# Strassen's seven products in the gated section of a decoder block with two attentions, with the last batch transposed on TensorE

## The chip, the core and the metric

The kernel runs on one core of a Trainium2 chip, in float32, as one launch. The metric is the device time of an execution in microseconds; the time of a kernel is the median of its runs. Five engines run their own queues of instructions: TensorE (PE, matrix products), VectorE (DVE), ScalarE (ACT), GpSimd (POOL) and SyncE (SP), which here issues all transfers.

## The reference, cut to what matters

There are 16 batches of 128 tokens with 512 features, and as many context tokens. A decoder block comes first: self-attention with 16 heads of 32, cross-attention on the context, and an MLP of 512 to 2048 to 512. A gated cross-attention follows, which is where the change lies. Its inputs are the block's result x and the context, normalised with a gain and an offset:

```python
Q, K, V = x @ Wq.T, a @ Wk.T, a @ Wv.T          # a = layer_norm(ctx); 16 heads of 32
scores = einsum(Q, K) * scale                   # scale = 1 / sqrt(32)
scores = where(mask, scores, -inf)              # mask: batch x key
out = softmax(scores) @ V
return x + tanh(gate) * (out @ Wo.T)
```

For a batch without a single valid key the softmax is undefined, and the result of the reference is not a number there. The inputs of the runs have all keys valid.

## The kernel before, in words

**Groups and sections.** The 16 batches form four groups of four (512 tokens). Each attention is done a group at a time, in sections: A0 to A3 (self), B0 to B3 (cross), then the MLP in 16 steps (4 groups by 4 quarters of the hidden width), then D0 to D3 (gated). x stays in SBUF, one tile for each group (`x[g]`).

**Steps.** `attend` runs a section in 16 steps, four for each batch; later stages of a batch lie some steps behind. A unit is one of the four parts of a batch's heads, 128x512 numbers. At the first step of a batch `scores` makes all four units on TensorE, into four PSUM banks called sc. Then, unit by unit, DVE adds the mask and moves the scores to SBUF (`scale_unit`) and takes a minimum (`least_unit`), ACT makes four exponentials with sums (`exp_unit`), DVE inverts the sums and POOL multiplies (`norm_unit`), DVE transposes in squares of 32 and SP stores the unit in device memory (`turn_unit`, the tile `away`), and SP loads pairs of units back in the order that the mixing wants (`receive_pair`, the tile `pT`). Eight to eleven steps after its scores, `mix` multiplies a batch's probabilities with the values (the bank `av`, copied by ACT into `mT`) and `out_project` makes the output chunk (`mo`), added into x by `finish`, which also stores the result.

**Beside the attention.** While section i attends, TensorE makes q, k and v of section i+1 (`jobs`, at the steps in PRODUCTS, three of four) and the inputs of section i+2 are made ready (`prepare`: hidden states and normalised context, transposed through device memory). A chunk is four matmuls of 128x512 into one bank, of which two (`pt`) and two single ones (`mm0`, `mm1`) are used in turn. In the self-attention, for three groups, the same projections are made by `block_product`: Strassen's method with seven products on a 2x2 split of both factors, each of four matmuls of 128x256, from sums of weight blocks and of token blocks made before (`left_blocks`, `right_blocks`), with copies and adds that build the four quarters of the result. The MLP works in that way, too (`H_ORDER` and `O_ORDER` give the order of the seven products). The q, k and v of D0 are chunks made before the gated sections begin.

**The gated sections.** D1 to D3 get q, k and v by plain chunks. The scale goes into q as ACT moves it out of its bank, and a column `mcol` of ones (not a number, where a batch has no valid key) into v. The mixed values of D0 to D2 are kept in SBUF, and their twelve output chunks are made beside the last section and shortly after its last scores, from the list `deferred`, since the last section has no section behind it whose projections could fill TensorE:

```python
return plan((deferred, [1, 3, 5, 7, 9, 11, 16, 17, 19]))
```

**Order.** Every engine's instructions stay in the order in which the program issues them (`InOrder`). Within a step that is: loads of probabilities, scores, what the step before left for later (`due`: evictions put off with `afterwards`), jobs, output chunk, mixing, preparations, transpose, normalisation, minimum and exponentials, masks of scores. All instructions are recorded in one helper, so every row of the trace is at line L49, and rows are told apart by the names of their tiles: `sc`, `av`, `mo`, `mm_q`, `mm_k`, `mm_v`, with the letter of the section (`_D`).

Of the kernel before, what the change touches and what calls it, by code (L numbers as in the profile page):

```python
# [16 lines left out]
P = 128  # L17
# [35 lines left out]
def decoder_then_gated_cross_attention(ctx: ExitStack, tc: tile.TileContext, a: dict, out: bass.AP):  # L53
# [120 lines left out]


    mrow8 = cpool.tile([NB, S], U8, tag="mrow8", name="mrow8")
    mrow = cpool.tile([NB, S], F32, tag="mrow", name="mrow")
    some = cpool.tile([NB, 1], F32, tag="some", name="some")
    mcol = cpool.tile([P, NB], F32, tag="mcol", name="mcol")
    gate = cpool.tile([P, 1], F32, tag="gate", name="gate")  # L180

    def load_small():
        nc.sync.dma_start(out=ms1, in_=a["mask_1x1xSxS2_fc1"][0, 0])
        nc.sync.dma_start(out=mrow8, in_=a["mask_BxS2_bf1"])
        nc.sync.dma_start(out=gate, in_=a["L1_xattn_gate"].partition_broadcast(P))

    def key_masks():
        nc.vector.tensor_copy(mrow, mrow8)
        nc.vector.tensor_reduce(some, mrow, AX.X, ALU.max)
        nc.vector.reciprocal(some, some)  # L190
        nc.vector.tensor_scalar(mrow, mrow, some, None, ALU.mult)
        tm = ps("mm", "tm")
        nc.tensor.transpose(tm[:, 0:NB], mrow, ident[0:NB, 0:NB])
        nc.vector.tensor_copy(mcol, tm[:, 0:NB])
# [4 lines left out]
    def small_jobs():  # L199
# [4 lines left out]
             lambda: turn_vectors(1), key_masks],  # L204
            [1, 2, 3, 8, 9, 13],
# [79 lines left out]
    def chunk_back(dst, back, k, scale=None, bias=None):  # L285

        dst, src = dst.rearrange("p (b n t) -> p b n t", b=GB, n=NQ), back[:, :, :, k].rearrange("p n b t -> p b n t")
        if scale is None:
            nc.scalar.copy(dst, src)
# [32 lines left out]
    def project_chunk(t, wt, actT, c, name, bias=None, bias0=0, bank="mm", scale=None):  # L322
# [4 lines left out]
        if bias is None:  # L327
            afterwards(
                "act", lambda: nc.scalar.copy(t[:, c], mm) if scale is None else nc.scalar.mul(t[:, c], mm, scale)
            )  # L330
# [3 lines left out]
    def values_chunk(v, wt, actT, b, name, bias_row=None, keep=None):  # L334
# [4 lines left out]
        if keep is None:  # L339
            afterwards("dve", lambda: nc.vector.tensor_tensor(v[:, b, :], mm, bias_row, ALU.add))  # L340
        else:
            afterwards("act", lambda: nc.scalar.mul(v[:, b, :], mm, keep[:, b : b + 1]))
# [17 lines left out]
    def left_blocks(wt, t):  # L360
# [3 lines left out]
        s3, s2, s4 = t  # L364
        return [a11, a12, s4, a22, a21, s2, s3], [
            (s3, a11, a21, ALU.subtract), (a21, a21, a22, ALU.add), (s2, a21, a11, ALU.subtract),
# [12 lines left out]
    def block_product(out, left, right, turned, name, bias=None):  # L379

        bank = {}
        (c11, c12), (c21, c22) = out

        def product(n, tag, first):
# [10 lines left out]
            return mm.rearrange("p (o t) -> p o t", t=HF)  # L397

# [35 lines left out]

    BLOCKS = (
# [12 lines left out]
        {12: (1,), 13: (6, 2), 14: (7, 5), 15: (4, 3)},  # L448
    )
# [11 lines left out]
    class Section:  # L461
# [4 lines left out]
        deferred = v_bias = None  # L466
# [4 lines left out]
    class Batch:  # L471
        def __init__(self, sec, b):
            self.sec, self.b, self.name = sec, b, f"{sec.name}_{b}"
            self.sc, self.s, self.mn, self.sum, self.away, self.pT = {}, {}, {}, {}, {}, {}
# [18 lines left out]
    def scale_unit(bt, j):  # L493
        s = work.tile([P, NQ, KC, Q], F32, tag="s", name=f"s_{bt.name}_{j}", bufs=8)
        bt.s[j] = s
# [30 lines left out]

    def receive_pair(bt, j):
# [10 lines left out]
    def mix(bt):  # L538
# [11 lines left out]
        def mixed_out():  # L550
            if sec.v_bias is None:
                nc.scalar.copy(mT.rearrange("p c q -> p (c q)"), av)
# [27 lines left out]
    def attend(sections, ready, others, after=None):  # L580
# [11 lines left out]
        def step(k, bt=None, jobs=(), ahead=None, last=True):  # L592
# [3 lines left out]
            if pair % 2 and 0 <= pair < len(units):  # L596
# [6 lines left out]
            if m == 0 and projected:  # L603
                before = projected.popleft()
                if before.sec.deferred is None or last:
                    out_project(before)
                else:
                    before.sec.deferred.append(lambda: out_project(before))
            done = k // GB - 2
            if m == 2 and 0 <= done < len(batches):  # L610
# [4 lines left out]
            if 0 <= k - 3 < len(units):  # L615
                turn_unit(*units[k - 3])
            if 0 <= k - 2 < len(units):
# [769 lines left out]
```

## Time and profile before

| | |
|---|---|
| time, median of three runs (1202.28, 1202.28, 1206.63) | 1202.28 us |
| the profiled execution's own time | 1202.3 us |
| its span | 1200.0 us |
| TensorE: matmuls busy, weight loads busy | 1165.7 us, 772.2 us |
| DVE, ACT, POOL busy | 745.7, 581.6, 603.8 us |
| first scores of D0, first of D1, of D2, of D3 | 970.26, 1020.98, 1073.02, 1125.06 us |
| last scores | 1163.49 us |
| moved by transfers | 249.18 MB |

Times within the profile are in microseconds from the start of the span. A busy time is the sum of the durations of an engine's instructions; TensorE's overlap a little, and the ends of its matmuls are modelled, so the distances from start to start say more than durations. In a timeline row, x8 are eight records: one float32 matmul leaves two, so a chunk has eight, and so has a product of four 256-wide matmuls. A number in brackets at the end of a row is the time that the engine idled before it, with the name of what it waited for.

### The profile page before, as it was taken

To read this page: it belongs to the slowest core of one execution; us is meant where nothing else is said; L and a number is where in the kernel's file an instruction comes from. 1 tells how busy PE (TensorE), PEld (TensorE's weight loads), DVE (VectorE), ACT (ScalarE), POOL (GpSimd) and SP (SyncE) were. 2 spreads that over 40 slices of the span, in tenths; PEclk is the share of its full clock that TensorE was granted. 3 is DMA by queue.
4 is the path that set the end of the run, shared out by engine and by line. 5 is a ranking of instruction groups with operands and counts; after the bars stand their busy time and mean duration, and the time that the engine had idled before them with its cause. 6 is when DMAs were issued, how large, how long until landed. Compare 5 with 4: busy or idle time off the path is not lost. (4 is left out here: it accounts for less than half of the span.)

```text
span 1200.0 us, 20209 instructions
## 1 busy us (share of the span) xinstructions
PE 1165.7 (97%) x6707; PEld 772.2 (64%) x6707; DVE 745.7 (62%) x1444; ACT 581.6 (48%) x2038; POOL 603.8 (50%) x555
## 2 busy tenths in 40 slices
PE   7989999999999999998999999999999999999997
PEld 5867677644444444444788888888888754444443
DVE  8678979776867767865754634542532255648674
ACT  2556667666655556664231222222222256868552
POOL 6777878675757556675233524433441232324231
PEclk9999999999999999999999999999999999999999
DMA  6578778898978869697696474585457538676576
GB/s 213 159 199 218 201 207 221 222 263 211 211 212 207 233 195 245 180 270 226 217 320 203 158 268 158 184 285 190 150 206 248 171 107 225 166 203 188 160 227 183
DMA packets 317983, 249.18 MB, mean 208 GB/s; under 512 B 82932, under 2 KB 278200, under 8 KB 313016
## 3 DMA queue, kind: packets, MB, share of 16 engines
q1 hardware_dynamic: 317840, 247.89, 70.9%
q8 instruction: 53, 0.87, 0.3%
q14 instruction: 50, 0.41, 0.1%
q10 hardware_dynamic: 40, 0.01, 0.0%
HBM read 158.70 MB, written 89.13 MB: 207 GB/s over the span
## 5 line engine op out<-in xcount | busy, mean ns | idle before, releaser
L49 ACT ACTIVATE s_B<-s_B,mn_B 128x128 f32<-128x128 f32 x256 | 99.5, 391 | 82.0 <-issue 60.6
L49 POOL TENSOR_TENSOR s_D<-s_D,sum_D 128x512 f32<-128x512 f32 x64 | 66.6, 1041 | 142.1 <-DVE sum_D L49 133.8
L49 DVE TENSOR_TENSOR h<-h,h 128x512 f32<-128x512 f32 x80 | 54.9, 687 | 119.0 <-PE h L49 118.4
L49 ACT ACTIVATE s_A<-s_A,mn_A 128x128 f32<-128x128 f32 x256 | 99.5, 393 | 55.7 <-issue 37.8
L49 ACT ACTIVATE s_D<-s_D,mn_D 128x128 f32<-128x128 f32 x256 | 99.4, 390 | 42.2 <-issue 34.6
L49 ACT ACTIVATE h<-h 128x512 f32<-128x512 f32 x64 | 40.3, 630 | 158.1 <-DVE h L49 153.8
L49 POOL TENSOR_TENSOR s_B<-s_B,sum_B 128x512 f32<-128x512 f32 x64 | 67.0, 1047 | 62.7 <-DVE sum_B L49 54.8
L49 POOL TENSOR_TENSOR s_A<-s_A,sum_A 128x512 f32<-128x512 f32 x64 | 66.7, 1043 | 53.9 <-DVE sum_A L49 49.6
L49 POOL TENSOR_TENSOR s_B<-s_B,mask 128x512 f32<-128x512 f32 x64 | 81.8, 1279 | 6.2 <-DVE s_B L49 4.6
L49 POOL TENSOR_TENSOR s_A<-s_A,ma 128x512 f32<-128x512 f32 x64 | 81.8, 1278 | 5.8 <-DVE s_A L49 4.3
L49 POOL TENSOR_TENSOR sh<-h 128x512 f32<-128x512 f32 x32 | 41.5, 1298 | 53.1 <-ACT h L49 43.3
L49 POOL TENSOR_TENSOR rstd_aD<-rstd_aD,mhalf 128x1 f32<-128x1 f32 x12 | 6.6, 550 | 115.1 <-DVE rstd_aD L49 101.8
L49 PE MATMUL mo_B<-w_co,mT_B 128*128 128x512 f32 x128 | 60.7, 618 | 1.8 <-ACT mT_B L49 1.8
L49 PE MATMUL h<-T_C,w 128*128 128x256 f32 x256 | 61.1, 381 | 1.2 <-DVE h L49 1.2
L49 PE MATMUL h<-T_C,t 128*128 128x256 f32 x256 | 60.7, 380 | 1.2 <-DVE h L49 1.1
L49 PE MATMUL mo_A<-w_ao,mT_A 128*128 128x512 f32 x128 | 59.1, 604 | 1.8 <-ACT mT_A L49 1.8
L49 PE MATMUL mo_D<-w_go,mT_D 128*128 128x512 f32 x128 | 57.9, 601 | 2.9 <-ACT mT_D L49 2.9
L49 PE MATMUL h<-sx,t 128*128 128x256 f32 x256 | 60.6, 379 | 0.0
L49 PE MATMUL o<-t,h 128*128 128x256 f32 x256 | 60.5, 379 | 0.0
L49 PE MATMUL o<-w,h 128*128 128x256 f32 x256 | 60.5, 379 | 0.0
L49 PE MATMUL o<-t,sh 128*128 128x256 f32 x256 | 60.5, 379 | 0.0
L49 PE MATMUL mm_v_D<-w_gv,T_a 128*128 128x512 f32 x128 | 59.9, 616 | 0.0
(220 smaller groups left out, 2753.1 us busy)
## 6 DMA issues: line engine op xcount, KB each, us to landing
t<-kept SPq DMA_DIRECT2D x24, 1024.0 KB, 10.2
away_A<-s_A SPq DMA_DIRECT2D x64, 256.0 KB, 2.7
pT_A<-away_A SPq DMA_DIRECT2D x128, 128.0 KB, 2.9
away_B<-s_B SPq DMA_DIRECT2D x64, 256.0 KB, 3.2
pT_B<-away_B SPq DMA_DIRECT2D x128, 128.0 KB, 3.1
away_D<-s_D SPq DMA_DIRECT2D x64, 256.0 KB, 3.0
pT_D<-away_D SPq DMA_DIRECT2D x128, 128.0 KB, 2.8
w<-in_L_xattn_w_dram SPq DMA_DIRECT2D x24, 512.0 KB, 4.3
```

The costliest lines, as they stand in the source:

```text
L49: return lambda *args, **kw: self.tc.keep_in_program_order(call(*args, **kw))
```

## The change

**Projections.** q, k and v of D1 to D3 come from `block_product`, at the steps of GATED_BLOCKS. Products 1, 6 and 7 share a bank (`mm0`) and accumulate: 6 begins when ACT has copied 1 out, and 7 when it has copied 6. The sums of the weight blocks are made once: those of Wq at the end of the MLP, of Wk on DVE and of Wv on POOL in the first steps of D0. The token sums are made on POOL for each group, four of the hidden states (in `prepare`, from step 10) and four of the context (steps 0 to 3 of the section before).

**Outputs.** The output chunks of D0, D1 and D2 become one block product for each group (`added_product`, DEFERRED_BLOCKS), added straight into x: ACT copies products 1, 6 and 7 into spare tiles and POOL adds them, DVE adds the other four from their banks. D3 keeps its four chunks. tanh(gate) is multiplied into Wo while that is prepared, and `finish` is a plain addition. Mixed values of D0 and D1 are stored in device memory (eight transfers of 256 KB) and fetched back in the steps 6 to 13 of D2's attention. x of the first group is stored in device memory during the MLP and fetched back at those steps 8 to 11; in between its tile holds block sums.

**Masks.** `mcol` and `key_masks` go. For each group `find_void` makes 0/max(mask) for each batch in an MLP step, and `add_void` adds that to x on ACT, 16 times (zero, or not a number for a batch with no valid key).

**Last batch.** The four units of the last batch of D3 are turned by TensorE, four transposes of 128x128 a unit into an sc bank, and copied out by DVE (even units) and ACT (odd ones), with no transfer; its mixing comes at step 67 in place of 70 and its output chunk in the step after. In the gated sections exponentials are issued ahead of normalisations.

**Around it.** The last two of the MLP's output products change places, and a small exponential near the MLP's end makes ACT load its table there.

```diff
@@ GatedAttention.jobs
-            keep = mcol[:, g * GB : (g + 1) * GB]
-            aT, xT = self.aT, self.xT
-            out = [lambda c=c: project_chunk(self.q, w["gq"], xT, c, f"q_{n}", scale=-SCALE) for c in range(KC)]
-            out += [lambda c=c: project_chunk(self.k, w["gk"], aT, c, f"k_{n}") for c in range(KC)]
-            out += [lambda b=b: values_chunk(self.v, w["gv"], aT, b, f"v_{n}", keep=keep) for b in range(GB)]
-            return plan((out, PRODUCTS), ([mask], [7]))
+            a_sides, a_sums = right_blocks(self.aT, self.a_at)
+            products = [
+                block_product(halves(self.q), self.sides[0], self.x_sides, False, f"q_{n}"),
+                block_product(halves(self.k), self.sides[1], a_sides, False, f"k_{n}"),
+                block_product(by_quarters(self.v), self.sides[2], a_sides, True, f"v_{n}"),
+            ]
...
+            if g == 1:
+                more = (
+                    ([by_dve(o) for o in self.sums[1]], [1, 1, 2, 2]),
+                    ([by_pool(o) for o in self.sums[2]], [4, 5, 6, 7]),
+                )
+            elif g == 3:
+                more = self.deferred_start()
+            return plan(
+                *blocks_plan(products, GATED_BLOCKS), ([by_pool(o) for o in a_sums], [0, 1, 2, 3]), ([mask], [9]), *more
+            )
@@ step: products of each projection, deferred group
+    GATED_BLOCKS = (
+        {0: (1,), 1: (6, 2), 2: (7,), 3: (5,), 4: (4,), 5: (3,)},
+        {5: (1,), 6: (6,), 7: (7, 2), 8: (5,), 9: (4,), 10: (3,)},
+        {11: (1, 2), 12: (6,), 13: (7, 5), 14: (4,), 15: (3,)},
+    )
+    DEFERRED_BLOCKS = (
+        {0: (1,), 1: (6, 2), 2: (7,), 3: (4,), 4: (5,), 5: (3,)},
+        {5: (1,), 6: (6, 2), 7: (7,), 8: (4,), 9: (5,), 10: (3,)},
+        {12: (1,), 13: (6, 2), 14: (7,), 15: (4,), 16: (5,), 17: (3,)},
+    )
@@ added_product
+            if n in (1, 6, 7):
+                t = parts[0]
+                parts.rotate(-1)
+                nc.scalar.copy(t, product(n, "mm0", n == 1))
...
+            elif n == 5:
+                add(c22, product(n, "mm1", True))
@@ deferred_start: steps of D2's attention
+                ([begin_sums], [11]),
+                ([lambda: add(self.o_sums) for _ in range(4)], [11, 12, 13, 14]),
+                ([lambda: add(self.m_sums[0]) for _ in range(4)], [12, 13, 14, 15]),
@@ last batch
+    def turn_by_array(bt, j):
+        s = by_head(bt.s.pop(j)).rearrange("p c n k -> p c (n k)")
+        tp = ps("sc", f"tp_{bt.name}_{j}")
+        for c in range(KC):
+            nc.tensor.transpose(tp[:, c * S : (c + 1) * S], s[:, c], ident)
@@ void
+        def find_void(self):
+            m8, self.void = self.load_mask(), void[:, self.g * GB : (self.g + 1) * GB]
+            def make():
+                nc.vector.tensor_reduce(self.void, m8, AX.X, ALU.max)
+                nc.vector.reciprocal(self.void, self.void)
+                nc.vector.tensor_scalar(self.void, self.void, 0.0, None, ALU.mult)
+            afterwards("dve", make)
...
+        if n % GB == 3 and r == 2:
+            gates[n // GB].find_void()
@@ mlp
-        O_ORDER = (0, 1, 3, 5, 6, 4, 2)
+        O_ORDER = (0, 1, 3, 5, 6, 2, 4)
```

## The prediction

> **What bounds the kernel now.** First the busy line of the page, then TensorE's waits from 950 us on, where the gated sections lie.
>
> ```profile
> PE 1165.7 (97%) x6707; PEld 772.2 (64%) x6707; DVE 745.7 (62%) x1444; ACT 581.6 (48%) x2038; POOL 603.8 (50%) x555
> ```
> ```profile
> engine line waited for: us in total, times, longest us
> PE mo_D L49 <- ACT mT_D L49: 2.9, 2, 2.2
> PE sc_D L49 <- DVE x L49: 1.4, 1, 1.4
> PE sc_D L49 <- DVE s_D L49: 0.7, 2, 0.3
> ```
> TensorE (PE) never rests: 5.0 us of waits in 250. The time there is the sum of its matmuls, so what counts is how many there are, how wide, and which new waits come between them. Its timeline gives one gated batch and the tail:
>
> ```profile
> 1009.27 7.13 PE L49 MATMUL mm_v_D<-w_gv,T_a 128*128 128x512 f32 x16
> 1016.34 1.08 PE L49 MATMUL av_D<-pT_D,v_D__7550 128*32 128x128 f32 x32
> 1017.35 3.70 PE L49 MATMUL mm_v_D<-w_gv,T_a 128*128 128x512 f32 x8
> 1020.98 1.17 PE L49 MATMUL sc_D<-k_D,q_D 32*128 32x128 f32 x32
> ...
> 1163.49 1.17 PE L49 MATMUL sc_D<-k_D,q_D 32*128 32x128 f32 x32
> ...
> 1175.10 7.13 PE L49 MATMUL mo_D<-w_go,mT_D 128*128 128x512 f32 x16 [2.17 <-ACT mT_D L49]
> ...
> 1192.49 3.70 PE L49 MATMUL mo_D<-w_go,mT_D 128*128 128x512 f32 x8 [0.73 <-ACT mT_D L49]
> ```
> Starts repeat every 12.81 us (1008.17, 1020.98): scores 1.11, mixing 1.02, three 512-wide chunks at 3.56. The chunks are q, k and v of the next section or, after 1125.06, deferred outputs. What takes their place exists already in the self-attention, four rows of whose timeline follow. The second fence, of the same view, has a group of transposes from the kernel's start and two places at the end of the cross-attention:
>
> ```profile
> 190.47 1.89 PE L49 MATMUL mm_q_A<-sums_A,w_sq 128*128 128x256 f32 x8
> 192.20 1.89 PE L49 MATMUL mm_q_A<-T_A,sums 128*128 128x256 f32 x8
> ...
> 221.35 1.89 PE L49 MATMUL mm_k_A<-T_A,sums 128*128 128x256 f32 x8
> 224.02 1.99 PE L49 MATMUL mm_v_A<-w_sv,sums_A 128*128 128x256 f32 x8 [0.78 <-DVE k_A L49]
> ```
> ```profile
> 6.30 1.12 PE L49 MATMUL tp_A<-ident,ln_A 128*128 128x128 f32 x4 [1.73 <-DVE ln_A L49]
> ...
> 530.97 1.07 PE L49 MATMUL av_B<-pT_B,v_B 128*32 128x128 f32 x28 [2.84 <-DMA pT_B<-away_B]
> 531.96 5.40 PE L49 MATMUL mm_v_D<-w_gv,T_a 128*128 128x512 f32 x8
> ...
> 548.99 5.40 PE L49 MATMUL mo_B<-w_co,mT_B 128*128 128x512 f32 x8 [1.80 <-ACT mT_B L49]
> ```
> A product of four 256-wide matmuls starts 1.73 us after the one before. The product at 224.02 waited for the eviction of an earlier bank: 2.67 us from start to start, a loss of 0.94. (The 5.40 rows serve a rival.)
>
> **Projections by seven products.** Twelve chunks (12×3.557 = 42.7 us) become 21 products. The self-attention's section with products, 169.48 to 230.61, takes 61.13 us; less scores and mixings (four of 1.11+1.02), outputs (four of 3.54) and 0.94 of stalls, 37.5 remain, 1.786 each. That saves 5.2 per section; the plain section after it (230.61 to 295.58, 64.97) against this one gives 4.8 without the stalls. I take 5.0, three times.
>
> The Trainium skill, "TensorE: Matmul & The Clock Gate", Back-to-back issue gap, says that weight loads and matmuls together set the spacing, with 81 ns sustained at 128 columns and 131 at 512. A line through these gives an estimate of 98 at 256, three quarters of a wide one: 21 products would then take 55 us, and every section would lose some 13. The trace disagrees, 1.73 against 3.56; the measurement decides.
>
> **New waits for a bank.** Products 1, 6 and 7 accumulate in one bank, and 6 and 7 must wait until ACT has copied it. Where PE has nothing in between, it stands still: 1→6 of q and 6→7 of v in each section, 6→7 of k in the first, 1→6 of deferred group 0; eight places. The nearest row, 224.02, lost 0.94 around a 0.69 us DVE add; a 0.57 us copy (ACT, k_D) instead gives 0.82. Bounds: 0, and 0.82+1.55 if four exponentials (0.39 each) stand ahead of the copy on ACT. I take 0.82: the copy is queued ahead of that step's exponentials. Eight cost 6.6.
>
> **Sums and adds.** Per section POOL gains eight sums (1.27 each), DVE twelve adds into q, k, v (0.69) while ACT loses three copies. In 1000–1050 DVE is busy 30.8 of 50 and POOL 15.7, so this is covered; uncovered, the DVE adds would be 8.3 us a section. The query-weight sums (one POOL, three DVE) and the gate's four multiplications go to the MLP's end, beside the last products of the MLP: nothing; were they late, the first product would stand behind 3×0.69. Four key-weight sums on DVE early in section one may take 1.75 instead of 0.69 (the MLP's t<-w beside a POOL sum took 1.75); I put 0.5 on scores there (0 to 4). In steps 11 to 15 of section three POOL has two sums and a normalisation, 1.27+1.27+1.04 = 3.6 us against about 2.9 of PE work; probabilities come up to 5×0.7 late, but are wanted three steps later: +1.0 (0 to 3.5).
>
> **Start of section one.** The last two output products of the MLP are swapped, so the bank that the first scores wait for (1.42) is emptied earlier: −1.4 (0 to −1.42).
>
> **Deferred outputs.** Of these, nine groups lie between 1125.06 and the last scores: 32.0 us become 14 products at 1.786, 25.0; plus one bank wait, 0.8, and 1.0 at a score bank in the second batch, where PE has some 7.5 us of work left against 9.3 on DVE (0 to 3): −5.2. Their mixed values, and the first group's x, now go through device memory, 256 KB each; the away_D stores of that size landed in 3.0 us, and the fetches start four or more steps ahead. SP has them among the away and pT transfers; no gated wait names a DMA, so none is charged (0 to 2, were a pT to arrive late). The x parts leave in an MLP step; SP holds weight loads there (512 KB in 4.3 us), which run about 8 us ahead, against some 3 us for one part. The copies of products go into spare tiles, from where POOL adds them into x (three copies, four POOL sums and four DVE adds a group; POOL 1.27 each, 12 in 38 us where it was busy 10.5): covered, and nothing on PE waits for the sums in x but the stores.
>
> **Tail.** After the last scores PE now does seven chunks and three mixings. It will do seven products (12.5), four chunks (14.2), three mixings (3.1), scores (1.1) and 16 transposes: from tp_A, 4×1.1 = 4.4. The 2.17 wait goes, since no transfer stands ahead of the last mixing; what is late next is the copy after it, 0.73 still. With the closing add that is 36.2 against 33.5 before (1163.49 to 1196.98): +2.7 (0 to +5).
>
> **Void keys.** 16 ACT additions (0.63) and four masks with three small DVE operations each come into the MLP, in place of scales on evictions that ACT did anyway. ACT idles 153.8 us there before h<-h, so the additions are covered; each is queued behind the TensorE group that it follows and ahead of the next T and h copies, where 0.63 is under the 2.2 us that the copies idle on average (158.1 over 64). DVE's three operations take under 0.3 us each by its 128x4 rows (a reciprocal 0.17), but they wait for a DMA, and the h additions are queued behind them: see the last rival. The small key-mask operations of the start, one transpose among them, go, at no price that the waits show.
>
> **Sum.** Section one −5.0+2.5−1.4+0.5 = −3.4; two and three −5.0+1.6 each = −6.8; POOL +1.0; deferred −5.2; tail +2.7: −11.7. The profiled run took 1202.3 us, span 1200.0 and 2.3 around it, which is the median of the runs, too. So 1190.6.
>
> **Rivals.**
> *Copies hidden.* The eight waits, the lag of POOL and of the score bank all vanish (6.6+1.0+1.0+0.5): 1181.5. Against: the order of PE's work is fixed and the pairs are adjacent.
> *Copies behind exponentials.* Each of the eight waits 1.55 longer: 12.4, 1203.0, no gain. For: ACT's exponentials of a unit are consecutive. Against: the order on ACT. It decides if a unit's minimum is early, by over half a step.
> *The clock.* After 2.84 us of idle a chunk took 5.40 instead of 3.70, after 1.80 again; after 2.17 at 1175.10 it did not, nor after 0.78 at 224.02. If each of the eight short waits costs that 1.7, 13.6 come on top: 1204.2. It decides from idles near 1.8 us. The Trainium skill, same page, section "A second HAM failure mode: psum-queue depth-cycling", says that frequent short idles between groups that cycle through PSUM banks make the clock gate oscillate. By that rule the sections would run at this rival's time; no row here shows it at 0.8 us.
> *Not faster: the masks.* In each of four MLP steps DVE waits until a mask has landed. In the trace one such wait was 9.0 us:
> ```profile
>   DMA m<-in_mask_BxS_bf_dram: 9.0, 1
> ```
> If all four stood in DVE's queue like that, beyond a slack of about 2.8 us, with h evictions behind them and PE behind those, 4×6.2 = 25: 1215, slower. It decides where the mask is issued: landing over 10 us after its issue. Against: the weight loads of those steps are issued 8 us ahead of their step.
> That the change does not do what it says: 512-wide mm_q_D rows would remain and the time stay; I give it nothing, the instructions being in the program.
>
> **How the numbers follow.** 0.5% (6.0 us) is about what a measurement of this kernel can tell from no change. Forecast, 1184 to 1196: 0.55. Copies hidden: 0.13. Behind exponentials 0.10, clock 0.08: both within 0.5% for the most part. Masks 0.08. The rest, 0.06, half slower. Faster 0.73, same 0.14, slower 0.13. From 1181 to 1205 leaves out the masks and a little on either side.
>
> **What would show it.** Right: product starts 1.73 apart; mm_q_D, mm_k_D, mm_v_D with waits of 0.6 to 0.8 on ACT, eight in all; the first scores of the sections 47 to 49 us apart; last scores near 1149. Wrong: waits over 2 us at these places (exponentials), 256-wide starts over 2 us with no wait (clock), h waiting for DVE behind m in the MLP, an av_D waiting for pT_D, or sc_D for s_D at every batch.

## The result, and the profile after

Over 22 runs of each kernel the median is 1197.35 us with the change and 1202.06 us before; the ratio is 0.9963, with a 95% interval of 0.9947 to 0.9978. So the change makes the kernel faster by 4.5 us (by the ratio; the medians lie 4.7 apart), a little over a third of the 11.7 that were forecast. The interval leaves out 1, but the gain is less than the 0.5% named as what can be told from no change. The profiled execution has a span of 1195.9 us against 1200.0: 4.1 us less, in keeping with the runs, so the two traces can be laid side by side.

The busy line of the page, then TensorE's waits from 930 us on (who waited for whom: total, times, longest). Besides the names explained above, `mm_o` are the products of the deferred outputs, `parts` the spare tiles that ACT copies them into, and `gsums` sums of weight blocks:

```profile
PE 1152.9 (96%) x7010; PEld 830.0 (69%) x7010; DVE 770.5 (64%) x1493; ACT 593.6 (50%) x2061; POOL 673.4 (56%) x612
```
```profile
PE av_D L49 <- DMA pT_D<-away_D: 2.7, 2, 2.2
PE sc_D L49 <- DVE s_D L49: 2.5, 2, 2.3
PE mm_q_D L49 <- ACT q_D L49: 2.3, 3, 0.8
PE mm_o_D L49 <- DVE x L49: 2.1, 1, 2.1
PE mm_v_D L49 <- ACT v_D L49: 2.0, 3, 0.7
PE mo_D L49 <- ACT mT_D L49: 0.9, 2, 0.8
PE mm_k_D L49 <- POOL gsums L49: 0.8, 1, 0.8
PE mm_o_D L49 <- ACT parts L49: 0.8, 1, 0.8
```
TensorE is busy for 12.8 us less, and 9.1 us more of the gated part are waits: 14.1 against 5.0. Six of them (mm_q, mm_v) and the ones of mm_k and mm_o_D for parts are the forecast waits for a bank, 0.7 to 0.8 each. (The list names POOL for mm_k; ACT's copy out of that bank ended within 0.1 us of POOL's sum.) Three others are over 2 us each: a mixing that waits for its probabilities, for which nothing was charged, and scores and a product that wait for DVE, for which 0.5 and 1.0 were. Here they are in the timeline of TensorE, with what follows the first two:

```profile
982.12 0.50 PE L49 MATMUL sc_D<-k_D__7653,q_D 32*128 32x128 f32 x6
984.95 1.12 PE L49 MATMUL sc_D<-k_D__7653,q_D 32*128 32x128 f32 x26 [2.33 <-DVE s_D L49]
986.00 1.99 PE L49 MATMUL mm_q_D<-x,w_gq 128*128 128x256 f32 x8
...
1055.27 1.71 PE L49 MATMUL av_D<-pT_D,v_D 128*32 128x128 f32 x28 [2.18 <-DMA pT_D<-away_D]
1056.91 4.71 PE L49 MATMUL mm_v_D<-w_gv,T_a 128*128 128x256 f32 x16
...
1154.77 1.99 PE L49 MATMUL mm_o_D<-gsums_o,mixed 128*128 128x256 f32 x8 [2.11 <-DVE x L49]
```
The mixing at 1055.27 took 1.71 in place of 1.07, and the two products after it 4.71 in place of 3.72 as at 1005.44; the granted clock was 0.66 from 1055 to 1060. So the wait cost 2.2, and the slow clock behind it 1.6 more. By the starts of the scores, the difference stands like this:

| part | before | after | change | forecast |
|---|---|---|---|---|
| first scores of D0 at | 970.26 | 971.16 | +0.9 | 0 |
| section one (to the first scores of D1) | 50.72 | 50.02 | −0.7 | −3.4 |
| section two | 52.04 | 52.45 | +0.4 | −3.4 |
| section three | 52.04 | 49.14 | −2.9 | −2.4 |
| deferred outputs (to the last scores) | 38.43 | 34.93 | −3.5 | −5.2 |
| last scores to the end of the span | 36.51 | 38.20 | +1.7 | +2.7 |
| sum | | | −4.1 | −11.7 |

Sections one and two are where most of the gain is missing (6.5 of 7.6 us). The first scores come between 964.9 and 971.9 in all the profiles below, though most of these kernels differ in nothing ahead of them; so +0.9 there means nothing, and profiles are compared from the first scores to the end of the span: 229.7 before, 224.7 after. A profile is one execution, and in the runs below it lies up to 3.5 us from the median of its kernel (e2 above it, e11 below); differences of that size in a profile's total say little by themselves.

### The profile page after: what moved, and what is told of

Its sections match the earlier page's. It is cut to its first block, busy times and chain, and to the rows that moved or that the text cites. A ratio compares the mean times of both kernels' runs of the same rounds, so it can differ in the third digit from the quotient of the medians.

```text
span 1195.9 us, 21040 instructions
## 1 busy us (share of the span) xinstructions
PE 1152.9 (96%) x7010; PEld 830.0 (69%) x7010; DVE 770.5 (64%) x1493; ACT 593.6 (50%) x2061; POOL 673.4 (56%) x612
## 4 chain that ended last, share of the span: by engine, by line
PE 82%; DVE 5%; DMA 4%; POOL 3%; issue 3%; SPq 2%; ACT 1%; ACTq 0%; DVEq 0%; POOLq 0%
PE o L49 15%; PE h L49 14%; PE mo_A L49 5%; PE mm_v_B L49 5%; PE mm_q_B L49 5%; PE mm_k_B L49 5%; PE mo_B L49 4%; PE mm_k_A L49 3%; PE mm_q_D L49 3%; PE mm_k_D L49 3%; PE mm_v_A L49 3%; PE mm_v_D L49 3%; PE mm_o_D L49 3%; PE mm_q_A L49 3%; SPq L49 2%
## 5 line engine op out<-in xcount | busy, mean ns | idle before, releaser
L49 ACT ACTIVATE s_D<-s_D,mn_D 128x128 f32<-128x128 f32 x256 | 99.5, 391 | 27.1 <-issue 10.6
L49 PE MATMUL mm_v_B<-w_cv,T_e 128*128 128x512 f32 x128 | 57.7, 599 | 0.0
L49 PE MATMUL mm_k_B<-T_e,w_ck 128*128 128x512 f32 x128 | 57.3, 595 | 0.0
```

The source lines that it names most:

```text
L49: return lambda *args, **kw: self.tc.keep_in_program_order(call(*args, **kw))
```

## The theories

**Suppliers late.** TensorE's work shrank as forecast, but probabilities (a way through device memory that SP issues and waits for) and DVE's evictions now come later than TensorE wants them. **Bank waits.** The waits between products 1, 6 and 7 cost more than forecast. A third, that the new masks in the MLP cost time, is tested by e12.

The trace of SP's queue speaks for the first. Its longest waits between 970 and 1190, first in the changed kernel, then in the one before:

```profile
SPq L49 <- DMA away_D<-s_D: 53.1, 26, 5.8
```
```profile
SPq L49 <- DVE s_D L49: 49.7, 35, 7.0
SPq L49 <- DMA away_D<-s_D: 29.4, 19, 3.4
```
Before, SP waited most for DVE to finish units, and 29.4 us for stores to land. Now it stands 53.1 us, up to 5.8 at once, for stores to land before it may issue the loads of probabilities. The longest is the cause of the wait at 1055, in SP's timeline of the changed kernel; the second fence has the stores and loads of the same batch in the kernel before:

```profile
1043.24 0.91 SPq L49 DMA_DIRECT2D back_x<-turned_x  x2
1044.26 0.93 SPq L49 DMA_DIRECT2D away_D<-s_D  x2
1051.00 1.74 SPq L49 DMA_DIRECT2D pT_D<-away_D  x4
```
```profile
1045.64 0.93 SPq L49 DMA_DIRECT2D away_D<-s_D  x2
1049.78 1.75 SPq L49 DMA_DIRECT2D pT_D<-away_D  x4
```
Two stores issued from 1044.26 on had landed only at 1051.0, 6.7 us later; the loads then had 1.7 us until TensorE wanted them at 1052.7. Before, the same two had landed after 4.1 us, and the loads had 5.8 us until the mixing at 1055.57. So the time in hand was lost on both sides: the landing took 2.6 us more, and TensorE came 1.5 us sooner after the stores (8.4 in place of 9.9).

## The experiments

Each ratio is to the kernel before. Those of the experiments come from five rounds with 4 to 12 runs of each kernel (e10 has 4); the two columns on the right come from one profile of each.

| run | ratio, 95% interval | first scores to end | waits over 1 us in the gated part, on |
|---|---|---|---|
| changed kernel | 0.9963, 0.9947 to 0.9978 | 224.7 | av 2.2, sc 2.3, mm_o 2.1 |
| e1, orders | 0.9954, 0.9937 to 0.9972 | 225.4 | av 3.3 and 2.1, sc 3.4, mm_o 2.1 |
| e2, key sums in the MLP | 0.9967, 0.9950 to 0.9983 | 228.7 | av 2.0, first sc 2.2, mm_o 2.1 |
| e3, not stored | 0.9904, 0.9883 to 0.9925 | 221.3 | sc 2.3, mm_o 2.1 |
| e4, orders, sums, five first | 0.9969, 0.9955 to 0.9982 | 229.2 | av 3.0, 2.3, 1.0; first sc 2.2; sc 2.5 |
| e5, not stored, orders | 0.9923, 0.9905 to 0.9942 | 223.7 | av 2.5, 1.0; sc 3.4, 2.5 |
| e6, 2 KB runs | 0.9963, 0.9944 to 0.9982 | 229.1 | av 3.3, sc 2.3, mm_o 2.1 |
| e7, orders, sums on POOL | 0.9960, 0.9940 to 0.9981 | 227.1 | av 2.9, 2.8, 1.7, 1.2; sc 2.6 |
| e8, last batch by transfer | 1.0013, 0.9992 to 1.0034 | 235.1 | av 5.1 and four of 1.3 to 1.7, sc 2.3, mm_o 2.1 |
| e9, mixing later | 0.9939, 0.9919 to 0.9959 | 221.7 | sc 2.3, mm_o 2.5 |
| e10, and key sums later | 0.9912, 0.9894 to 0.9931 | 221.6 | mm_k 1.6 and 1.4, mm_o 2.5 |
| e11, and orders | 0.9924, 0.9899 to 0.9950 | 218.0 | mm_k 2.0, 1.2; av 2.2; sc 2.9 |
| e12, void left out | 0.9980, 0.9962 to 0.9997 | 225.1 | av 2.1, 1.1; sc 2.3; mm_o 2.1 |
| e13, and balanced | 0.9907, 0.9888 to 0.9925 | 219.9 | mm_k 1.4, mm_o 2.3, 1.6 |
| e14, before, mixing later | 0.9991, 0.9975 to 1.0007 | 228.7 | first sc 1.4, mo 2.3 and 1.3 |
| e15, later, not stored | 0.9921, 0.9901 to 0.9941 | 221.3 | mm_k 1.6, 1.4; mm_o 2.5, 1.6 |
| e16, balanced and orders | 0.9934, 0.9910 to 0.9957 | 220.9 | av 2.7, 1.0; mm_k 1.4; mm_o 2.3 |

**e1: another product in between.** Within a step, products are taken as written after 1, in place of 1, 6 and 7 first.

```diff
-        {0: (1,), 1: (6, 2), 2: (7,), 3: (5,), 4: (4,), 5: (3,)},
-        {5: (1,), 6: (6,), 7: (7, 2), 8: (5,), 9: (4,), 10: (3,)},
-        {11: (1, 2), 12: (6,), 13: (7, 5), 14: (4,), 15: (3,)},
+        {0: (1,), 1: (2, 6), 2: (5,), 3: (7,), 4: (4,), 5: (3,)},
+        {5: (1,), 6: (6,), 7: (2, 7), 8: (5,), 9: (4,), 10: (3,)},
+        {11: (1, 2), 12: (6,), 13: (5, 7), 14: (4,), 15: (3,)},
...
-        {0: (1,), 1: (6, 2), 2: (7,), 3: (4,), 4: (5,), 5: (3,)},
+        {0: (1,), 1: (2, 6), 2: (7,), 3: (4,), 4: (5,), 5: (3,)},
...
```


> Only the order of the seven products is changed, so that another product stands between 1 and 6 and between 6 and 7 of every projection, and between 1 and 6 of the first deferred group. If the eight waits for a copied bank carry the missing gain (theory: bank waits), the waits of mm_q_D, mm_k_D, mm_v_D and mm_o_D for ACT go from 5.9 us to under 0.5, and with a start lost beside each (2.74 from start to start in place of 1.83) the span falls by 6 to 8 us against the changed kernel: ratio to the kernel before about 0.990. If the suppliers are what is late (theory: DVE, and transfers), TensorE only comes earlier to the scores and mixings and waits there instead: the waits of sc_D for DVE and of av_D for pT_D rise from 5.2 to 8 or more, and the span falls by under 3 us: ratio about 0.994.

The waits of q, k and v for a bank are gone altogether, 5.1 us of them (the deferred group's 0.8 stayed), and the time moved by 0.1%, within the interval. What was won went to the suppliers: av_D now waits 5.4 us, sc_D 3.4, and the clock fell behind two of these three waits. From TensorE's timeline of this run:

```profile
979.46 2.04 PE L49 MATMUL sc_D<-k_D__7653,q_D 32*128 32x128 f32 x26 [3.37 <-DVE s_D L49]
981.43 3.78 PE L49 MATMUL mm_q_D<-x,w_gq 128*128 128x256 f32 x8
...
1050.65 1.82 PE L49 MATMUL av_D<-pT_D,v_D 128*32 128x128 f32 x28 [3.26 <-DMA pT_D<-away_D]
1052.40 4.60 PE L49 MATMUL mm_v_D<-w_gv,T_a 128*128 128x256 f32 x16
```
So waits for banks, taken alone, are not what the gain is missing by.

**e2: key-weight sums in the MLP's last step**, on DVE.

```diff
-                    ([by_dve(o) for o in self.sums[1]], [1, 1, 2, 2]),
...
+            if r < 4:
+                nc.vector.tensor_tensor(*sec.sums[1][r])
```


> Only the four sums of the key weights move, from DVE in the first three steps of the first gated section to DVE in the last step of the MLP. If they are why the second scores of that section waited 2.33 us for DVE (theory: DVE late), that wait falls under 0.5 and the span by about 2; ratio to before about 0.9945. If DVE is late there for another reason (the evictions of the MLP's last products, the new adds into q), the wait stays above 1.5 and the time does not move. If the sums delay the MLP's last evictions instead, the first scores wait and nothing is won.

The third outcome: the wait at the second scores went, and the first scores waited 2.2 us for DVE's evictions of the MLP, with a product of 3.78 us in place of 1.9 behind them. DVE has no room at either place.

**e3: mixed values not stored.**

```diff
-            nc.sync.dma_start(out=gated[key][:, :, b * S : (b + 1) * S], in_=bt.mT)
+            pass
...
-                fetch_part(f"mT_D{g}", mixed[g], n)
+                nc.sync.dma_start(out=mixed[g][:, n], in_=gated["x0"][:, n])
```


> The mixed values of the first two groups are not stored (8 transfers of 256 KB left out), and what is fetched in their place is the stored x of the first group, in as many bytes; so the deferred outputs of two groups are computed from other numbers. If the stores crowd the transfers (theory: transfers late), the DMA share between 1020 and 1070 falls from 0.86 towards 0.78, the 2.18 us wait of av_D for pT_D near 1055 goes, the slow matmuls after it (4.71 for two products in place of 3.7) too, and the span falls by 3 to 4: ratio about 0.993. If the wait is there because TensorE reaches the mixing sooner, whatever else is moved, it stays above 1.5 us and the time within 1 us.

av_D waits for no transfer any more, sections two and three take 48.24 and 48.65 us, and the ratio is 0.9904, its interval clear of the changed kernel's. (The runs are 7.1 us faster than the changed kernel's, the profile from the first scores on 3.4; how much of the rest is spread of the runs is open.) The DMA share between 1020 and 1070 did not fall (0.86, as more is done in the same 50 us), so it isn't the mean share that decides. How soon the stores land fits better: SP's longest wait for them went from 5.8 to 3.3 us, all of these waits from 53.1 to 44.0.

**e4: orders, sums in the MLP, and product 5 ahead of 4** in the deferred groups. One of the three groups is shown; the other edits are those of e1 and e2.

```diff
...
-        {5: (1,), 6: (6, 2), 7: (7,), 8: (4,), 9: (5,), 10: (3,)},
+        {5: (1,), 6: (6, 2), 7: (7,), 8: (5,), 9: (4,), 10: (3,)},
...
```


> The orders of the first of these runs and the key-weight sums of the second together, and in the deferred groups product 5 ahead of product 4, so that DVE has two more products' time to empty the bank that product 3 needs (2.11 us of waiting near 1154). If bank waits, DVE at the start and DVE in the deferred groups are separate and add up: 7 + 2.3 + 2.1, some 11 us less than the changed kernel, ratio about 0.987. If the transfers take over as the limit (theory: transfers late), the waits of av_D for pT_D grow from 2.7 to over 6 and the ratio stays above 0.991.

Nothing adds up: av_D waits 8.6 us in seven places, and DVE's 2.1 us have moved from mm_o_D to the next scores (2.5). The transfers have taken over, the second outcome of the expectation.

**e5: e1's orders, five first, not stored.**

```diff
+        {0: (1,), 1: (2, 6), 2: (5,), 3: (7,), 4: (4,), 5: (3,)},
...
+        {5: (1,), 6: (6, 2), 7: (7,), 8: (5,), 9: (4,), 10: (3,)},
...
-            nc.sync.dma_start(out=gated[key][:, :, b * S : (b + 1) * S], in_=bt.mT)
+            pass
...
```

> The orders of the products (another product between 1, 6 and 7; product 5 ahead of 4 in the deferred groups), and the mixed values of two groups not stored, as before (so the deferred outputs of two groups come from other numbers). With the stores, the orders alone moved the time by 0.1%, though they took away some 5 us of waits for banks. Theory transfers late: without the stores the orders pay, at least half of the 6 us: ratio to before 0.986 or lower, av_D waiting for pT_D under 2 us. If what was won by the orders is lost to DVE at the scores in the same way, or to transfers even without the stores, the ratio stays near 0.990 and waits of sc_D or av_D of 4 us or more appear.

Between the two: av_D still waits 3.8 and sc_D 5.9. Even without stores the orders won nothing (0.9923, against 0.9904 without stores and in the old orders).

**e6: runs of 2 KB**, the tiles in SBUF and in device memory with a batch's numbers together.

```diff
-            gated[key] = dram.tile([P, KC, TG], F32, tag=f"kept_{key}", name=f"kept_{key}")
-            nc.sync.dma_start(out=gated[key][:, :, b * S : (b + 1) * S], in_=bt.mT)
+            gated[key] = dram.tile([P, GB, KC, S], F32, tag=f"kept_{key}", name=f"kept_{key}")
+            nc.sync.dma_start(out=gated[key][:, b], in_=bt.mT)
...
```

> The mixed values are stored and fetched a batch at a time in runs of 2 KB in place of 512 B; as many bytes, a quarter of the packets. If the stores crowd the transfers by their number of packets, half or more of the 6 to 7 us that leaving them out gave comes back: ratio about 0.993 or lower, and away_D lands sooner (SP waits for it 53 us between 970 and 1190 in the changed kernel, 44 without stores). If bytes are what counts, the ratio stays at 0.996 and SP's wait at 50 or more.

No change in time, and SP's wait is 55.6. In this profile the late mixing stands in section three (3.3 us) and not in section two. So it isn't the number of packets of these stores.

**e7: e4's orders, sums of query and key weights on POOL in the MLP's last step.**

```diff
...
-            else:
-                nc.vector.tensor_tensor(*sec.sums[0][r - 3])
+            if 1 <= r < 4:
+                nc.gpsimd.tensor_tensor(*sec.sums[0][r])
+            elif r > 3:
+                nc.gpsimd.tensor_tensor(*sec.sums[1][r - 4])
```

The last key-weight sum follows at step 1 of D0.

> The orders again, and all sums of query and key weights on POOL in the last step of the MLP, so that DVE has neither at the start of the first gated section. Theory DVE late at the start: the wait at the first or second scores (2.2 to 3.4 us in all kernels so far) goes, with 1 to 2 us of slow matmuls after it: from the first scores to the end 225 becomes 221, ratio about 0.992. If POOL comes late with the query sums, mm_q_D waits for gsums instead. If transfers set the pace of the sections, what is won at the start is lost at av_D.

No wait over 1 us at the start; 10.2 us at av_D in seven places in their stead. The last sentence of the expectation is what happened. (One of the query sums overwrites a quarter of Wq, here ahead of the last chunks of D0's q, which read it. So q of the first group, and the result with it, come out as other numbers; the instructions and their sizes stay what the text says.)

**e8: the last batch through device memory again**, as before the change.

```diff
-            self.by_array = sec.at_end and b == GB - 1
+            self.by_array = False
...
-            elif m == 2 and 0 <= done < len(batches) - ready:
+            elif m == 2 and 0 <= done < len(batches):
```

> Only the turning of the last batch on TensorE is undone: its four units go through device memory, and its mixing and output come at steps 70 and 72 again. By the prediction's tail the transposes cost 4.4 us and saved 2.2; measured they took 0.53 a unit, 2.1 in all. If TensorE had to wait for the last transfers as before (2.2 us, and a longer end for lack of work beside it), this kernel is 1 to 3 us slower than the changed one: ratio 0.997 to 0.999. If transfers late is right, the last batch's four stores and eight loads also crowd those before, and it is slower by 3 or more. If it is no slower, the part was worth nothing.

Slower than the changed kernel by 0.5%, all of the change's gain: the last mixing waits 5.1 us for its transfer, and from the last scores to the end it takes 45.2 us in place of 38.2. So TensorE's transposes are worth some 7 us at the end of the profile, and 6 in the runs.

**e9: the mixing a step later.** This attacks lateness itself and leaves all transfers in place.

```diff
-            if projected and (m == 0 or ready and bt is None):
+            if projected and (m == (1 if ready else 0) or ready and bt is None):
...
-            elif m == 2 and 0 <= done < len(batches) - ready:
+            elif m == (3 if ready and bt is not None else 2) and 0 <= done < len(batches) - ready:
```


> In the gated sections each mixing, and the output or store behind it, comes one step later (about 3 us), except for the last two batches; nothing else is moved. Theory transfers late: with one step more for the way through device memory the waits of av_D for pT_D (2.7 us in the changed kernel, 4 to 10 in others) and the slow matmuls after them go; 3 to 5 us less than the changed kernel, ratio 0.992 to 0.994, about what leaving out the stores gave. If the transfers cannot keep up in the mean (share 0.86), the lag grows from batch to batch, and av_D waits again by the second or third section: ratio 0.996.

No av_D waits for a transfer at all, at a share of 0.89. The two stores that were late at 1051 land no sooner here: they are issued from 1042.79 on, and the loads behind them go out at 1048.64, 5.9 us later; but the mixing comes at 1055.28 and finds its probabilities. Sections two and three take 48.46 us each. The ratio is 0.9939; its interval overlaps that of the changed kernel, so the time alone does not settle it. The trace does, and e3, which moves no step and has nearly the same sections.

**e10: and the key-weight sums at steps 3, 4, 5 and 9**, with the edit of e9.

```diff
-                    ([by_dve(o) for o in self.sums[1]], [1, 1, 2, 2]),
+                    ([by_dve(o) for o in self.sums[1]], [3, 4, 5, 9]),
```

> The same, and the four key-weight sums on DVE in the steps 3, 4, 5 and 9 of the first gated section in place of 1, 1, 2 and 2 (the products need them from step 6 on). Theory DVE late at the start: the wait of 2.3 us at the second scores goes, and up to 2 us of slow matmuls after it, so 2 to 4 us less than the run above: ratio 0.989 to 0.992. If the MLP's last evictions are what DVE is late with, the wait stays at over 1.5.

0.9912, 10.6 us faster than before and clear of the changed kernel's interval. Its windows over sections two and three (us; busy and count of PE, PEld, DVE, ACT, POOL; clock, DMA share, GB/s) beside those of the changed kernel:

```profile
1014.20:1062.67 48.47, 46.26 (x429) 38.53 (x425) 38.76 (x78) 37.49 (x151) 26.56 (x24) 1.00 0.92 244
1062.67:1111.13 48.46, 46.25 (x429) 38.52 (x425) 37.78 (x77) 33.34 (x143) 30.45 (x28) 1.00 0.88 251
```
```profile
1021.18:1073.63 52.45, 48.83 (x425) 39.62 (x424) 39.12 (x77) 37.28 (x150) 26.48 (x24) 0.97 0.86 228
1073.63:1122.77 49.14, 47.21 (x426) 38.44 (x425) 39.02 (x77) 33.74 (x144) 31.47 (x29) 1.00 0.87 249
```
The same work in 48.47 us in place of 52.45, at a higher DMA share and a full clock. What the sums gained is less plain: the wait at the second scores is gone, but two products of k wait 1.6 and 1.4 us, and section one takes 49.26 against 49.49 in e9. The two intervals overlap.

**e11: and the orders** of e1 and e4, with the edit of e10.

> Both of these, and the orders that keep another product between those that share a bank, and product 5 ahead of 4. With suppliers no longer late, the waits for banks (5.9 us in eight places, about 1 us of start to start each) are no longer hidden behind something else: another 4 to 6 us, ratio 0.984 to 0.988. If DVE or the transfers take over again, as they did when the orders were changed alone, the ratio is that of the run above.

Another 3.5 us in the profile, none in the runs (0.9924): the waits of q and v for banks are gone, others are back (av 2.2, sc 2.9).

**e12: void left out.**

```diff
-                gates[3].add_void(p - GB)
...
-            afterwards("act", lambda: gates[(n - 5) // GB].add_void((n - 5) % GB))
...
-            gates[n // GB].find_void()
```

> The masks for batches without a valid key are left out: no mask loads and small DVE operations in the MLP, no 16 additions to x on ACT (with the inputs used they add zero). If they cost nothing, as predicted, the time is that of the changed kernel, 0.996. If one of the four masks, or the additions, hold up the MLP, it is faster by the waits of h for DVE and more: 2.8 us in the changed kernel against 2.3 before, so by 0.5 to 1 us, less than a measurement can tell, but the profile can.

No faster: 0.9980 against 0.9963, with intervals that overlap. The masks cost nothing that can be told, as forecast. The rival that had DVE wait for their landing did not occur: in the changed kernel no wait of DVE in the MLP is put down to one of these four loads.

**e13: the deferred batches balanced.** Mixing later, sums at 2, 3, 4 and 8, and:

```diff
-        {5: (1,), 6: (6, 2), 7: (7,), 8: (4,), 9: (5,), 10: (3,)},
+        {5: (1,), 6: (6, 2), 8: (7,), 9: (5,), 10: (4,), 11: (3,)},
...
```


> Mixing a step later, key-weight sums at the steps 2, 3, 4 and 8, and in the second deferred group the products from 7 on a step later, 5 ahead of 4, so that the third batch of the last section has four products beside it in place of three and the second five in place of six. If DVE sets the pace of that third batch (its adds and evictions take about 9.5 us against 7.6 us of matmuls), the wait of 2.1 to 2.5 us there goes without another in its place: 2 to 3 us less than with later mixing and sums alone, ratio about 0.989, first to last scores under 181 us (183.0 there). If it is a single late bank, the wait turns up at the next scores again, and the ratio stays 0.991.

First to last scores take 179.9 us (183.0 in e10), as expected, but the ratio of 0.9907 lies nearer to the other outcome and can't be told from e10's 0.9912. The reason did not come out: 1.2 of the 3.1 us lie in section one, where the sums stand a step earlier. The second batch of the last section is 1.7 us shorter, by the product that it lost, and the third no longer by the one that it gained (11.8 against 11.9), but mm_o_D still waits 2.3 us for DVE in it. What went is the slow product behind the wait, 3.61 in e10 and 1.92 here, and that may be chance (see the counts at the end). So it is not the lack of matmuls alone that makes DVE late there.

**e14: the kernel before, mixing later.**

```diff
-            if m == 0 and projected:
+            if projected and m == (1 if ready and bt is not None else 0):
...
-            if m == 2 and 0 <= done < len(batches):
+            if m == (3 if ready and bt is not None else 2) and 0 <= done < len(batches):
```

> The kernel before, with its gated mixings a step later and nothing else. There no mixing waited for a transfer. If later mixing wins only by hiding late transfers, it wins nothing here: ratio 0.999 to 1.001. If it wins by another way (DVE or ACT order, banks), the ratio is 0.998 or lower.

0.9991, an interval that holds 1, as expected for late transfers. But the profile shows that two effects cancel here. Sections two and three take 50.45 us each in place of 52.04: a mixing now stands right ahead of the next scores, so that three chunks on end take 10.50 us from start to start in place of 10.70 with a mixing among them, and the waits at the second scores (0.33 each) are gone. From the last scores to the end it takes 39.60 in place of 36.51, since the last outputs come later, too. So this run does not show by itself that a step's delay wins nothing but lateness. For the changed kernel that rests on e3 and e9: sections without a late transfer take 48.24 and 48.65 us without the delay and 48.46 with it.

**e15: later, and not stored**: the edits of e10 and of e3.

> Mixing a step later, key-weight sums at the steps 3, 4, 5 and 9, and the mixed values of two groups not stored (the deferred outputs of two groups come from other numbers). Without later mixing, leaving out the stores gave 6 to 7 us. If that was the lateness of the probabilities alone, it gives nothing now: ratio 0.991, as with the stores. If the stores cost by themselves, some 3 us or more come on top: 0.988.

0.9921 against 0.9912 with the stores, and no av_D waits. With a step of slack the stores cost nothing that can be told, so what they cost the changed kernel was, as far as these runs can tell, lateness alone. SP waits 53.6 us for landings here, and 40.9 in e14, with no mixing late in either: the total of these waits does not say by itself that something is late.

**e16: e13 with the orders of q, k and v.**

> The first of these four with another product between those that share a bank, in q, k and v. With transfers, start and deferred batches out of the way, the seven waits for banks are all that is left: 1 us each from start to start, 5 to 7 us, ratio 0.983 to 0.985. If av_D or sc_D wait in their place, suppliers have no more to give at this pace, and the ratio stays above 0.988.

0.9934. The waits of q, k and v for banks are gone but for 0.4 us, and av_D waits 3.7 again with slow matmuls behind it. Five times (e4, e5, e7, e11, e16) the orders were tried on top of something else, and no time came of it.

## Why the prediction was wrong

**What held.** The products: with no late transfer a section takes 48.24 and 48.65 us in e3 and 48.46 in e9, where 48.6 was forecast (52.04−5.0+1.6). In e9, less scores and mixings (8.5) and three waits for banks (2.2; the changed kernel has two), that is 1.80 for a product, 1.786 in the forecast. The waits for banks: 0.68 to 0.77 of idle; one costs 2.74 from start to start in place of 1.83, 0.9 (0.82 forecast). The masks: nothing, though one of DVE's three operations took 0.68 us and not under 0.3, and ACT's additions 0.71 and not 0.63. What did not come is POOL's lag in section three (1.0 forecast): the mixings that it should delay waited for nothing.

**The step that failed** is the one on transfers, "no gated wait names a DMA, so none is charged"; the sign of being wrong that the forecast names, an av_D waiting for pT_D, is what came. The wait list of the kernel before shows which transfers were late, not by how little the others were in time. Each pair of units goes out, lands, and comes back in a fixed number of steps; the change makes those steps 7% shorter and puts four more stores of 256 KB into section two (192 GB/s became 228 between 1020 and 1070). SP's waits for landings grew from 29.4 to 53.1 us, and the landing at 1051 took 2.6 us more than before, for a mixing that came 1.5 us sooner after the stores. So section two paid 2.18 us of waiting and 1.6 of slow clock: 3.8 of the 7.6 us that are missing. e3 (nothing stored) and e9 (one step more) each take this wait away and bring the section to 48.2 and 48.5 us, and e15 finds no further gain from both; e14 adds nothing to this. The upper bound that I gave, 2 us, was for one wait; with the clock it took 3.8.

**The second is a term too small**: 0.5 for the key-weight sums at the start, with 4 as its bound, measured 2.33, in a section that is 2.7 us short of its forecast. DVE's timeline shows it:

```profile
975.21 1.76 DVE L49 TENSOR_TENSOR gsums<-w_gk 128x512 f32<-128x512 f32 x1
977.00 1.64 DVE L49 TENSOR_TENSOR w_gk<-w_gk 128x512 f32<-128x512 f32 x1
...
981.55 0.67 DVE L49 TENSOR_TENSOR gsums<-w_gk 128x512 f32<-128x512 f32 x1
982.26 0.69 DVE L49 TENSOR_TENSOR gsums<-w_gk,gsums 128x512 f32<-128x512 f32 x1
```
The first two, beside POOL's token sums (975.15 to 979.8), took 1.7 each, the other two, with POOL idle, 0.7. The Trainium skill, "SBUF — State Buffer", Who interferes with whom, says that a DVE instruction with two SBUF inputs contends with a GpSimd instruction that reads SBUF; these rows agree. The four take 4.8 us of a queue that must also empty four score banks in some 11 us, and in which DVE is busy 99% of the time (4.97 of 5 us from 975 to 980 and from 980 to 985). Taking them away took the wait away (e2, e7, e10), but other waits came, and the time hardly moved.

**The third** is the batch of the last section with the least matmuls, the third of its four: 1.0 at a score bank was forecast from 7.5 us of TensorE work against 9.3 on DVE, and 2.11 measured, at the bank of a product. That DVE would be late there was right, the size was half; e13 gave the batch one product more and the wait stayed at 2.3, so the reason is at best part of it.

**The tail** went the other way: the nearest row, tp_A, gave 1.1 for four transposes; they took 0.43 to 0.65, 2.0 in all and not 4.4. The row lay at the very start of the kernel, with records of 421 ns against 273 here at the same granted clock of 1.00; what slows them there wasn't tried. The tail cost +1.7 and not +2.7. Its sum was short, too: the terms named there, with the wait of 0.73 and the closing add of 0.75, come to 36.8 and not 36.2. And what the transposes save was priced at the wait of 2.17 alone: with transfers late, e8 shows 7 us in the profile.

**The rivals.** That the copies are hidden, and that exponentials hold them up: neither; the waits were as forecast. The clock came true in another form. It didn't fall after the eight short waits, but after some of those of over 2 us. Windows of e1, around the wait at 979.46:

```profile
975.00:980.00 5.00, 1.63 (x18) 1.11 (x20) 4.97 (x10) 2.34 (x13) 1.19 (x2) 0.91 0.29 89
980.00:985.00 5.00, 5.00 (x34) 4.06 (x27) 3.76 (x8) 4.35 (x19) 4.51 (x5) 0.50 0.56 153
```
So this late supplier was paid nearly twice: 3.4 us of idle, then some 2.7 us lost at half clock (scores and product 979.46 to 985.00).

**What stays open.** Why orders that take away 5 us of waits never show in the runs: each time other waits took their place in the profile (av_D, sc_D, the clock), but which of them one would have to cure, and whether DVE's order in the last section could be changed so that none comes, was not found. What is missing in section one beyond the 1.8 us of the second term (0.9 of 2.7) is not accounted for either. With the step and the sums moved, e10 is 10.6 us faster than the kernel before; that this comes near the 11.7 does not make the forecast right, since that kernel is another one.

## What to carry to other kernels

Where an engine is 97% busy and its work is cut, list for each supplier how early it is now, in steps and in us, before counting the gain; a wait list shows only what is late already. A fixed distance in steps between a store and the use of what comes back gets shorter with every us taken from a step, so lengthen it with the same edit: one step more took away the late transfers here (e9: 0.9939), and with the key-weight sums moved as well most of the missing gain was back (e10: 0.9912). Removing short waits paid nothing here, as a later wait on another supplier swallowed them each time.

## What the runs showed of the hardware

TensorE's clock fell after many of the idle times of 2.0 to 3.4 us, not after all: after 2.18 at 1055 the next five microseconds ran at a clock of 0.66, and in e1 after 3.37 at 0.50, but after 2.33 at 984.95 and 2.11 at 1154.77 in the changed kernel the products that followed kept 1.83 to 1.93. Waits of 0.7 to 0.8, eight in 200 us, never did it. Counted over the eighteen profiles (idle times of TensorE between 60 and 1180 us, and the granted clock of the 5 us after each), the clock fell, to 0.50 to 0.71, after 7 of 67 idle times of 0.95 to 2.0 us, the shortest of 1.53; after 15 of 35 of 2.0 to 2.4; and after 38 of 46 of 2.4 to 3.5. So a wait of 2.0 to 2.4 us cost nothing more in some places and slow matmuls in others (1.6 us of them at 1055); what decides between the two was not found. The Trainium skill, "TensorE: Matmul & The Clock Gate", Why this matters for your kernels, names gaps of about 3 us as the limit; in these traces 1.5 to 2.2 was at times enough. Of its second failure mode, frequent short idles between groups, nothing was seen at 0.8 us.
